# A graph attention kernel on one core: the maxima of heads 2 and 3 made apart, over four passes

## The chip, the core and the metric

The kernel runs on one core of a Trainium2 chip. The metric is the device time of one execution in microseconds (us); lower is better. TensorE multiplies matrices, VectorE, ScalarE and GpSimd do the element-wise work, and DMA queues move data between DRAM and the on-chip memory. In the profile they are PE (weight loads: PEld), DVE, ACT and POOL; SP is SyncE, which here only issues DMAs.

## The reference

Four layers follow each other on 1250 nodes of 1024 features: a graph attention with four heads, a block-sparse feed-forward layer with a large projection, a graph convolution, and a mixture of experts. Each has a layer norm ahead of it and is added to x. The change lies in the attention, which is

```python
def _L0_gnn_ref(h, W, a_l, a_r, src, dst):
    N, IN_FEAT, OUT_FEAT, HEADS, E = (1250, 1024, 256, 4, 20000)
    z = jnp.einsum('ni,hif->nhf', h, W)
    el = jnp.einsum('nhf,hf->nh', z, a_l)
    er = jnp.einsum('nhf,hf->nh', z, a_r)
    e = jax.nn.leaky_relu(el[src] + er[dst], 0.2)
    m = jax.ops.segment_max(e, dst, num_segments=N)
    ex = jnp.exp(e - m[dst])
    s = jax.ops.segment_sum(ex, dst, num_segments=N)
    alpha = ex / s[dst]
    out = jax.ops.segment_sum(alpha[:, :, None] * z[src], dst, num_segments=N)
    return out.reshape(N, HEADS * OUT_FEAT)
```

with h the layer norm of x. The maximum m of a destination node and head is the leaky ReLU of (the largest el over its sources, plus its er), since the leaky ReLU is monotonic.

## The kernel before

**The data.** The 1250 nodes are ten tiles (T) of 125 (R). The 20000 edges become a dense matrix of counts: CT holds it on chip with sources on the partitions, and nm_d in DRAM holds, for each tile of destinations, a mask of 125 destinations by 1250 sources that is 0 where there is an edge and -1e30 where there is none. Z holds the transformed features, with a column of ones behind each head's 256; Z of heads 0 and 1 lies in the buffer BZ, that of heads 2 and 3 in a tile of its own. el and er are the two halves of the scores.

**Maxima and bounds.** `maxima` (L336) goes over the ten tiles of destinations. For each it loads a tile nm of the mask (two DMAs on SP's queue, L106 and L107, 610 KB), and for both heads of a pair VectorE adds el, spread over the partitions (els), to the mask and takes the largest: one fused operation, L343, of 125 x 1250 for a head. It is a generator that stops after each, so that its work can be laid between other work. `bounds` (L347) turns the maxima of a pair of heads into two numbers for each destination (bd), which stand for the score less the maximum on the two branches of the leaky ReLU. `to_row` (L178) turns them by a TensorE transpose (L181) and a ScalarE copy to st (L183), and sends them to DRAM on POOL's queue (L185); `spread` (L188) loads them back, the same 2500 numbers for all 125 partitions (L190, 1220.7 KB), into rows[h], the tile rr. There are two rr buffers: head 2 takes the one of head 0, head 3 that of head 1.

**A pass.** `attend(h, b)` (L438) makes head h for the half b of the destinations, 625 of them. For each of ten source tiles, VectorE makes u from the rows and el (L443), ScalarE takes its exponential (L444), VectorE limits it and multiplies by the counts to w (L447), and TensorE multiplies w by Z into five accumulators of 125 x 257 (L449; in the profile each matmul of 32-bit data is two). At the end ScalarE copies the five sums of weights (L453), VectorE inverts them (L455, L456) and adds the scaled result to X (L459), which frees the accumulators: there are six, and a pass takes five. u and w have three buffers each.

The passes stand in the order (0,0), (0,1), (1,0), (1,1), (2,0), (3,0), (2,1), (3,1). `between` is stepped after each source tile of a pass:

```python
        with tc.tile_pool(name="mx1", bufs=1) as mxp:
            els1 = el_rows(1, mxp, tps)
            attend(0, 0)
            search = maxima(1, mxp, els1)
            attend(0, 1, search)
            attend(1, 0, search)
            bounds(1, mxp, tps, rowp)
            attend(1, 1)
```

So the 20 maxima of the second pair are made beside passes (0,1) and (1,0), one for each source tile, and the bounds of both heads follow together. The pool mx1 (nm, sc, els, top, bd, st) ends behind (1,1); the pool al, opened ahead of (2,0), holds the small tiles of the next layer norm (the statistics L503 among them) and takes the same memory.

**What sets the order.** The program's order isn't the order on the engines: a scheduler lays the instructions of each engine into one fixed queue when the kernel is built, and semaphores join the queues. An instruction waits for everything ahead of it on its own engine, a DMA for everything ahead of it on its issuing queue. SP's queue carries the mask tiles, and the weights of the projection (`load_weights`, L407) and of its small block-diagonal factors, the rails (`load_rails`, L412: maker L414 and up L415), which go into BZ as soon as heads 0 and 1 no longer need it. POOL's queue carries X, els, the rows of bounds and the products of the rails (L416, L418). TensorE multiplies the rails (L424). Behind the attention come the projection's matmuls (L595) by two levels of Strassen's scheme, then the graph convolution and the experts.

Of the kernel before, what the change touches and what calls it, by code (L numbers as in the profile page):

```python
# [8 lines left out]
F32 = mybir.dt.float32  # L9
# [10 lines left out]
P = 128  # L20
R, T = 125, 10
N = R * T
RA = 112
D = 1024
KD = D // P
# [10 lines left out]
NP = N + 2  # L36
NQ = NP // 4
HN, HT = N // 2, T // 2
# [60 lines left out]
def gnn_ffn_kernel(ctx, tc, x, src, dst, gat_w, a_l, a_r, maker, up, cproj,  # L99
# [98 lines left out]
    with tc.tile_pool(name="gw", bufs=1) as gwp, tc.tile_pool(name="gps", bufs=3, space=PSUM) as psp:  # L198
# [137 lines left out]
        def maxima(g, mxp, els):  # L336

            for d in range(T):
                nm = mxp.tile([R, N], F32, name="nm2", bufs=3 - g)
                dma(nc.sync, nm, nm_d[d])  # L340
                for h in (2 * g, 2 * g + 1):
                    sc = mxp.tile([R, N], F32, name="sc2")
                    nc.vector.tensor_tensor_reduce(sc, nm, els[:, h - 2 * g, :], scale=1.0, scalar=-3.0e38,  # L343
                                                   op0=ALU.add, op1=ALU.max, accum_out=mx[:, h, d:d + 1])
                    yield

        def bounds(g, pool, psp, rowp):  # L347

            hs = slice(2 * g, 2 * g + 2)
            for dst_t, f in ((el2, SLOPE), (el8, 1.0 - SLOPE)):  # L350
                nc.vector.tensor_scalar(dst_t[:, hs], el[:, hs], f, None, op0=ALU.mult)
            top = pool.tile([R, 2, T], F32, name="top")
            nc.vector.tensor_tensor(top, mx[:, hs], er[:, hs], op=ALU.add)
            nc.vector.scalar_tensor_tensor(top, top, SLOPE, top, op0=ALU.mult, op1=ALU.max)
            bd = pool.tile([R, 2, 2, T], F32, name="bd")
            nc.vector.tensor_tensor(bd[:, :, 0], er[:, hs], top, op=ALU.subtract)
            nc.vector.scalar_tensor_tensor(bd[:, :, 1], er[:, hs], SLOPE, top, op0=ALU.mult, op1=ALU.subtract)
            for h in range(2):
                rows[2 * g + h] = rowp.tile([R, 2, N], F32, name="rr", bufs=2)
                if 2 * g + h == 0:  # L360

                    for i in range(2):
                        for t0 in range(0, T, 4):
                            n = min(4, T - t0)
                            pb = psp.tile([P, 4, R], F32, name="pt")
                            for t in range(n):
                                nc.tensor.transpose(pb[:R, t, :], bd[:, h, i, t0 + t:t0 + t + 1].to_broadcast([R, R]),
                                                    ident[:R, :R])
                            copy = nc.vector.tensor_copy if t0 == 4 else nc.scalar.copy
                            copy(rows[0][:, i, t0 * R:(t0 + n) * R], pb[:R, :n, :].rearrange("p a b -> p (a b)"))  # L370
                    continue
                spread(rows[2 * g + h].rearrange("p a n -> p (a n)"),
                       to_row(pool, psp, bd[:, h].rearrange("p a t -> p (a t)"), 2 * T, f"bd{2 * g + h}"))
# [4 lines left out]
        with tc.tile_pool(name="mx0", bufs=1) as mxp:  # L378
            search = maxima(0, mxp, els0)
# [4 lines left out]
            bounds(0, mxp, psp, rowp)  # L384
# [50 lines left out]
    with tc.tile_pool(name="att", bufs=3) as atp, tc.tile_pool(name="aps", bufs=6, space=PSUM) as aps, \  # L435
# [25 lines left out]

        with tc.tile_pool(name="mx1", bufs=1) as mxp:
            els1 = el_rows(1, mxp, tps)
            attend(0, 0)
            search = maxima(1, mxp, els1)
            attend(0, 1, search)
            attend(1, 0, search)
            bounds(1, mxp, tps, rowp)
            attend(1, 1)
# [5 lines left out]
        xT = xTp.tile([P, KD, NP], F32, name="xT")  # L475
        for c in (HN, NP - 1):
            nc.gpsimd.memset(xT[:, :, c:c + 1], 0.0)
        with tc.tile_pool(name="al", bufs=2) as lnp:
            attend(2, 0)
# [770 lines left out]
```

## Time and profile before

| | us |
|---|---|
| median of 3 runs | 2926.47 (2922.64 to 2928.51) |
| the profiled execution | 2923.05, span 2921.3 |
| PE busy | 2857.7 (98%) |
| DVE busy | 1686.0 (58%) |
| ACT busy | 875.8 (30%) |
| POOL busy | 765.4 (26%) |
| 80 u (L443), attention only | 68.4, one 0.871 |
| 80 w (L447) | 64.3, one 0.809 |
| 20 maxima (L343) of heads 2 and 3 | 29.3, one 1.463 |
| 800 matmuls of the passes (L449) | 185.1 |

The busy time of an engine is the time from an instruction's start to its end, and successive instructions overlap a little, so starts are a better measure of a stretch than durations. A row of the timeline has the start, the length, the engine, the line, the operation with what it writes and reads, the number of instructions merged, and in brackets the engine's idle time ahead of it with what ended it. In the chain of work that ended last each step is followed back to what released it. The profile drops the digits of tile names, so nm2 is nm and sc2 is sc.

### The profile page before, as it was taken

What the parts mean: (1) busy time and instruction counts of PE and PEld (TensorE: products, weight loads), DVE (VectorE), ACT (ScalarE), POOL (GpSimd) and SP (SyncE); (2) the same over time, 40 slices, a digit from 0 to 9 for tenths busy, and PEclk for the clock granted to TensorE, in tenths of its full rate; (3) what the DMA queues carried; (4) which work ended last, traced back from release to release, by engine and by line L of the source; (5) the groups of instructions that cost most, each with busy time, mean ns of one, the idle gap of its engine ahead of it and who ended that gap; (6) DMA issues with size and microseconds to landing.
All of it is one profiled execution on the core that took longest, in us unless ns stands there. A gap on an engine that the chain in (4) does not pass through costs nothing.

```text
span 2921.3 us, 32800 instructions
## 1 busy us (share of the span) xinstructions
PE 2857.7 (98%) x11389; PEld 1892.0 (65%) x11389; DVE 1686.0 (58%) x2796; ACT 875.8 (30%) x1415; POOL 765.4 (26%) x994
## 2 busy tenths in 40 slices
PE   8999889999999999999999999999999999999998
PEld 5574777666766666666666667667667644445774
DVE  7686987855555565565465556455457665431114
ACT  2221234443343343343343443443440010010000
POOL 2000110224334334334334334344331100002001
PEclk9999999999999999999999999999999999999999
DMA  5245632569999999999999999999996502332655
GB/s 144 66 107 142 160 75 96 193 161 190 195 187 222 199 188 221 197 190 230 183 186 224 182 190 197 174 172 182 167 249 183 158 11 70 94 114 68 218 198 167
DMA packets 288438, 478.33 MB, mean 164 GB/s; under 512 B 75807, under 2 KB 159865, under 8 KB 287639
## 3 DMA queue, kind: packets, MB, share of 16 engines
q0 software_dynamic: 116176, 273.68, 52.9%
q1 hardware_dynamic: 172088, 202.44, 23.8%
q8 instruction: 95, 1.56, 0.2%
q14 instruction: 79, 0.65, 0.1%
HBM read 193.66 MB, written 282.34 MB: 163 GB/s over the span
## 4 chain that ended last, share of the span: by engine, by line
PE 80%; DMA 3%; DVE 2%; issue 0%; ACT 0%; POOL 0%; SPq 0%; DVEq 0%; ACTq 0%
PE po L595 55%; PE pab L1041 6%; PE ph L998 5%; PE po L866 4%; PE pz L429 3%; PE po L449 3%; PE po L1147 2%; DMA X<-in_gcn_w 2%; DMA yg<-ys_d,back 1%; PE pt L156 1%; PE pg L962 1%; DMA low<-in_gcn_w 1%; DMA rowbd<-st 0%; PE px L737 0%; PE pt L1137 0%
## 5 line engine op out<-in xcount | busy, mean ns | idle before, releaser
L608 POOL DMA_DIRECT2D acc_d<-low x686 | 594.6, 867 | 923.5 <-ACT low L604 895.6
L604 ACT COPY low<-po 128x626 f32<-128x626 f32 x735 | 501.2, 682 | 996.3 <-PE po L595 826.8
L595 PE MATMUL po<-X,arena 128*128 128x313 f32 x2144 | 603.5, 428 | 0.0
L595 PEld LDWEIGHTS po<-X,arena 128*128 128x128 f32 x2144 | 401.9, 189 | 170.2 <-issue 18.8
L595 PE MATMUL po<-low,arena 128*128 128x313 f32 x1584 | 449.2, 428 | 0.2 <-DVE low L588 0.2
L595 PEld LDWEIGHTS po<-low,arena 128*128 128x128 f32 x1584 | 296.8, 189 | 124.7 <-issue 13.2
L595 PE MATMUL po<-X,first_w 128*128 128x313 f32 x824 | 235.0, 429 | 0.9 <-DVE X L588 0.9
L595 PEld LDWEIGHTS po<-X,first_w 128*128 128x128 f32 x824 | 154.1, 189 | 67.0 <-issue 8.5
L595 PE MATMUL po<-X,BZ 128*128 128x313 f32 x648 | 185.8, 430 | 0.0
L588 DVE TENSOR_TENSOR X<-X 128x626 f32<-128x626 f32 x130 | 105.8, 816 | 111.1 <-PE po L595 88.2
L595 PE MATMUL po<-low,first_w 128*128 128x313 f32 x576 | 164.2, 428 | 0.9 <-DVE low L588 0.9
L595 PE MATMUL po<-low,BZ 128*128 128x313 f32 x552 | 158.4, 429 | 0.0
L595 PEld LDWEIGHTS po<-X,BZ 128*128 128x128 f32 x648 | 122.1, 191 | 50.7 <-issue 5.5
L212 PE MATMUL pz<-W,xT 128*125 128x512 f32 x320 | 141.2, 596 | 0.1
L595 PEld LDWEIGHTS po<-low,first_w 128*128 128x128 f32 x576 | 108.1, 189 | 45.8 <-issue 3.8
L595 PEld LDWEIGHTS po<-low,BZ 128*128 128x128 f32 x552 | 103.2, 189 | 44.5 <-issue 6.0
L588 DVE TENSOR_TENSOR X<-X,low 128x626 f32<-128x626 f32 x100 | 81.3, 814 | 79.8 <-PE po L595 65.2
L280 PE MATMUL pc<-os,od 125*125 125x417 f16 (+1 forms) x588 | 110.8, 344 | 4.9 <-issue 4.7
L449 PE MATMUL po<-BZ,w 125*125 125x257 f32 x400 | 95.6, 398 | 19.9 <-DVE w L447 18.8
L998 PE MATMUL ph<-low,first_w 125*125 125x512 f32 x250 | 109.5, 593 | 0.8 <-POOL tri L1066 0.8
L588 DVE TENSOR_TENSOR X<-low,X 128x626 f32<-128x626 f32 x88 | 70.9, 810 | 63.7 <-PE po L595 61.7
L588 DVE TENSOR_TENSOR low<-X,low 128x626 f32<-128x626 f32 x88 | 72.1, 820 | 60.6 <-PE po L595 59.6
(311 smaller groups left out, 3533.0 us busy)
## 6 DMA issues: line engine op xcount, KB each, us to landing
acc_d<-low POOLq DMA_DIRECT2D x735, 313.0 KB, 6.7
arena<-in_cproj SPq DMA_DIRECT2D x148, 256.0 KB
w<-in_w SPq DMA_DIRECT2D x16, 1024.0 KB
BZ<-in_cproj SPq DMA_DIRECT2D x56, 256.0 KB
first_w<-in_cproj SPq DMA_DIRECT2D x52, 256.0 KB
nm<-nm_d SPq DMA_DIRECT2D x20, 546.9 KB
w3t<-in_w SPq DMA_DIRECT2D x8, 1024.0 KB
X<-acc_d SPq DMA_DIRECT2D x19, 313.0 KB
```

The lines of the kernel that those rows point to most:

```text
L212: nc.tensor.matmul(pz, xT[:, k, t * R:(t + 1) * R], W[g][:, k], start=(k == 0), stop=(k == KD - 1))
L280: nc.tensor.matmul(pc[:, b, :nn], od[:, d - near[c][0], :], os[:, n0:n0 + nn], start=(c == win[d][0]), stop=(c == win[d][-1]))
L429: nc.tensor.matmul(pz, [*rail_parts(k)][-1][rows, :], xT[rows, (2 * b + k) % KD, n * NQ:(n + 1) * NQ], start=True, stop=True)
L449: nc.tensor.matmul(po[i], w[:, i * R:(i + 1) * R], Z[h // 2][:, s, h % 2, :], start=(s == 0), stop=(s == T - 1))
L588: tt(view(k), *a, op=ALU.add if sign == "+" else ALU.subtract)
L595: nc.tensor.matmul(po[:, o, :NQ], view(x)[:, q, o * P:(o + 1) * P], view(y)[:, q, :], start=(i == q == 0), stop=(i + 1 == len(pairs) and q ...
L604: nc.scalar.copy(part, po[:, :, :NQ])
L608: sent[:] = [nc.gpsimd.dma_start(out=acc_d[p - 1, i - 1], in_=part, accum_op=ALU.add).ins]
L866: nc.tensor.matmul(ph, block(a, x)[:, k, :], XS[W3[y, k]].rearrange("p q o -> p (q o)"), start=(k == 0), stop=(k == 3))
L998: nc.tensor.matmul(pa, cs[:, c, :], Y[FACTORS[p][1]][:, c], start=(c == 0), stop=(c == HT - 1))
L1041: nc.tensor.matmul(pab[:, :nn], w12[:, i, k, f * P:(f + 1) * P], rhs[:, k, n0:n0 + nn], start=(k == 0), stop=(k == KD - 1))
L1147: nc.tensor.matmul(po[:m, g, :], hid[:, f, s * P:s * P + m], w3t[:, f, g * 512:(g + 1) * 512], start=(f == 0), stop=(f == 1))
```

## The change

`maxima` now takes a list of heads instead of a pair, and so does `bounds`. Heads 0 and 1 are still made together. Heads 2 and 3 are made one by one: `search(2)` is stepped beside passes (0,1) and (1,0), with two steps for each maximum, and head 2's bounds follow behind (1,0); `search(3)` is stepped beside (1,1) and (2,0), two steps for each of its first five maxima and one for each of the others, so that head 3's bounds are written out after the sixth source tile of (2,0). Each head loads the ten mask tiles for itself: 20 loads of 610 KB in the place of ten. els and the two nm buffers stay as they were. The pool mx1 is now held to the end of (2,0), and the pool al is opened behind it; the tile xT and its two memsets, which came between the two pools, now come inside mx1.

```diff
@@ -333,55 +333,56 @@
                                                  start=(c == 0), stop=(c == EC - 1))
                         finish(d, pc)
 
-        def maxima(g, mxp, els):
+        def maxima(heads, mxp, els, bufs=2):
 
             for d in range(T):
-                nm = mxp.tile([R, N], F32, name="nm2", bufs=3 - g)
+                nm = mxp.tile([R, N], F32, name="nm2", bufs=bufs)
                 dma(nc.sync, nm, nm_d[d])
-                for h in (2 * g, 2 * g + 1):
+                for h in heads:
                     sc = mxp.tile([R, N], F32, name="sc2")
-                    nc.vector.tensor_tensor_reduce(sc, nm, els[:, h - 2 * g, :], scale=1.0, scalar=-3.0e38,
+                    nc.vector.tensor_tensor_reduce(sc, nm, els[:, h % 2, :], scale=1.0, scalar=-3.0e38,
                                                    op0=ALU.add, op1=ALU.max, accum_out=mx[:, h, d:d + 1])
                     yield
 
-        def bounds(g, pool, psp, rowp):
-
-            hs = slice(2 * g, 2 * g + 2)
+        def bounds(heads, pool, psp, rowp):
+
+            n = len(heads)
+            hs = slice(heads[0], heads[0] + n)
             for dst_t, f in ((el2, SLOPE), (el8, 1.0 - SLOPE)):
                 nc.vector.tensor_scalar(dst_t[:, hs], el[:, hs], f, None, op0=ALU.mult)
-            top = pool.tile([R, 2, T], F32, name="top")
+            top = pool.tile([R, n, T], F32, name="top")
             nc.vector.tensor_tensor(top, mx[:, hs], er[:, hs], op=ALU.add)
             nc.vector.scalar_tensor_tensor(top, top, SLOPE, top, op0=ALU.mult, op1=ALU.max)
-            bd = pool.tile([R, 2, 2, T], F32, name="bd")
+            bd = pool.tile([R, n, 2, T], F32, name="bd")
             nc.vector.tensor_tensor(bd[:, :, 0], er[:, hs], top, op=ALU.subtract)
             nc.vector.scalar_tensor_tensor(bd[:, :, 1], er[:, hs], SLOPE, top, op0=ALU.mult, op1=ALU.subtract)
-            for h in range(2):
-                rows[2 * g + h] = rowp.tile([R, 2, N], F32, name="rr", bufs=2)
-                if 2 * g + h == 0:
-
-                    for i in range(2):
+            for i, h in enumerate(heads):
+                rows[h] = rowp.tile([R, 2, N], F32, name="rr", bufs=2)
+                if h == 0:
+
+                    for j in range(2):
                         for t0 in range(0, T, 4):
-                            n = min(4, T - t0)
+                            w = min(4, T - t0)
                             pb = psp.tile([P, 4, R], F32, name="pt")
-                            for t in range(n):
-                                nc.tensor.transpose(pb[:R, t, :], bd[:, h, i, t0 + t:t0 + t + 1].to_broadcast([R, R]),
+                            for t in range(w):
+                                nc.tensor.transpose(pb[:R, t, :], bd[:, i, j, t0 + t:t0 + t + 1].to_broadcast([R, R]),
                                                     ident[:R, :R])
                             copy = nc.vector.tensor_copy if t0 == 4 else nc.scalar.copy
-                            copy(rows[0][:, i, t0 * R:(t0 + n) * R], pb[:R, :n, :].rearrange("p a b -> p (a b)"))
+                            copy(rows[0][:, j, t0 * R:(t0 + w) * R], pb[:R, :w, :].rearrange("p a b -> p (a b)"))
                     continue
-                spread(rows[2 * g + h].rearrange("p a n -> p (a n)"),
-                       to_row(pool, psp, bd[:, h].rearrange("p a t -> p (a t)"), 2 * T, f"bd{2 * g + h}"))
+                spread(rows[h].rearrange("p a n -> p (a n)"),
+                       to_row(pool, psp, bd[:, i].rearrange("p a t -> p (a t)"), 2 * T, f"bd{h}"))
 
         rows = {}
         rowst = ExitStack()
         rowp = rowst.enter_context(tc.tile_pool(name="rowp", bufs=1, side="right"))
         with tc.tile_pool(name="mx0", bufs=1) as mxp:
-            search = maxima(0, mxp, els0)
+            search = maxima((0, 1), mxp, els0, 3)
             for t in range(T):
                 for _ in range(3):
                     next(search, None)
                 z_tile(1, t)
-            bounds(0, mxp, psp, rowp)
+            bounds((0, 1), mxp, psp, rowp)
 
     XX = ctx.enter_context(tc.tile_pool(name="xpool", bufs=1)).tile([P, T, D], F32, name="X")
     X = XX[:R]
@@ -459,24 +460,33 @@
                 end = nc.vector.scalar_tensor_tensor(xs, po[i][:, :F], rs[:, i:i + 1], xs, op0=ALU.mult, op1=ALU.add)
             return end
 
+        def search(h, mxp, els):
+
+            for i, _ in enumerate(maxima((h,), mxp, els)):
+                yield
+                if i < 5 or h == 2:
+                    yield
+            bounds((h,), mxp, tps, rowp)
+
         with tc.tile_pool(name="mx1", bufs=1) as mxp:
             els1 = el_rows(1, mxp, tps)
             attend(0, 0)
-            search = maxima(1, mxp, els1)
-            attend(0, 1, search)
-            attend(1, 0, search)
-            bounds(1, mxp, tps, rowp)
-            attend(1, 1)
+            two, three = search(2, mxp, els1), search(3, mxp, els1)
+            attend(0, 1, two)
+            attend(1, 0, two)
+            next(two, None)
+            attend(1, 1, three)
 
             nc.vector.tensor_reduce(dis, deg.rearrange("p d s -> p s d"), AX.X, ALU.add)
             nc.vector.tensor_scalar(dis, dis, 1.0, None, op0=ALU.add)
             nc.scalar.activation(dis, dis, AF.Sqrt)
             nc.vector.reciprocal(dis, dis)
-        xT = xTp.tile([P, KD, NP], F32, name="xT")
-        for c in (HN, NP - 1):
-            nc.gpsimd.memset(xT[:, :, c:c + 1], 0.0)
+            xT = xTp.tile([P, KD, NP], F32, name="xT")
+            for c in (HN, NP - 1):
+                nc.gpsimd.memset(xT[:, :, c:c + 1], 0.0)
+            attend(2, 0, three)
+            next(three, None)
         with tc.tile_pool(name="al", bufs=2) as lnp:
-            attend(2, 0)
             nc.gpsimd.memset(m8, 1.0)
             nc.gpsimd.affine_select(m8, m8, pattern=[[-16, 8]], compare_op=ALU.is_ge, fill=0.0, base=0,
                                     channel_multiplier=1)
```

## The prediction

> **What bounds the kernel now.** First the page's chain of work that ended last, then the part of the span that the edit touches. Eight attention passes, each one head and one half of the destination nodes, run from 287 to 503 us.
>
> ```profile
> PE 80%; DMA 3%; DVE 2%; issue 0%; ACT 0%; POOL 0%; SPq 0%; DVEq 0%; ACTq 0%
> PE po L595 55%; PE pab L1041 6%; PE ph L998 5%; PE po L866 4%; PE pz L429 3%; PE po L449 3%; PE po L1147 2%; DMA X<-in_gcn_w 2%; DMA yg<-ys_d,back 1%; PE pt L156 1%; PE pg L962 1%; DMA low<-in_gcn_w 1%; DMA rowbd<-st 0%; PE px L737 0%; PE pt L1137 0%
> ```
>
> TensorE sets the end; the later work (L595 on) queues behind the attention, so time gained or lost before 503 us moves the end one for one. The stretches, one by one, show where attention itself isn't TensorE's:
>
> ```profile
> 330.00:378.00 48.00, 36.31 (x144) 27.86 (x142) 48.00 (x74) 10.45 (x22) 0.00 (x0) 0.93 0.38 106
> 378.00:403.00 25.00, 22.71 (x101) 18.43 (x102) 20.94 (x35) 9.81 (x15) 2.08 (x4) 1.00 0.66 165
> 431.00:454.00 23.00, 22.17 (x100) 18.58 (x100) 18.63 (x28) 8.47 (x16) 0.00 (x0) 1.00 0.00 1
> ```
>
> Columns: length, then busy time of PE, PEld, DVE, ACT, POOL, then PE clock, DMA share, GB/s. The third stretch is a pass that TensorE bounds: 23.0 us, VectorE busy 18.6. In the first VectorE has no gap: the 20 maxima of heads 2 and 3 (L343) lie there. The timeline around its end and the next stall:
>
> ```profile
> 374.34 1.47 DVE L343 CUSTOM_DVE_ANT_0 sc<-nm,els 125x1250 f32<-125x1250 f32 x1
> 376.51 0.19 DVE L353 TENSOR_TENSOR top<-mx,er 125x20 f32<-125x20 f32 x1
> 379.26 0.25 ACT L183 COPY st<-pt 20x125 f32<-20x125 f32 x1 [0.87 <-PE pt L181]
> 379.80 0.52 POOL L185 DMA_DIRECT2D rowbd<-st  x1 [66.97 <-ACT st L183]
> 381.90 0.53 POOL L190 DMA_DIRECT2D rr<-rowbd  x1 [1.59 <-DVE X L459]
> 392.87 0.69 DVE L503 BATCH_NORM_STATS2 st<-X 125x6 f32<-125x512 f32 x1 [3.95 <-DMA rowbd<-st]
> 407.40 0.85 PE L424 MATMUL pt<-BZ 128*128 128x128 f32 x4 [1.49 <-POOL BZ L418]
> 431.22 22.29 PE L449 MATMUL po<-Z,w 125*125 125x257 f32 x100 [0.92 <-DVE X L459]
> ```
>
> The reader is to see the trip of a head's bounds through DRAM (L183, L185, L190), a VectorE stop of 3.95 us and a rails stop of 1.49. From the second matmul of pass (0,1), 318.84, to that of (3,0), 431.22, are 112.4 us; four passes at 23.0 are 92.0. So 20.4 us is lost here, and that is all that can be won.
>
> **The change, part by part.** The built order of the instructions shows that it touches nothing before the fix-ups of pass (0,0) but two tiny VectorE operations, hidden in VectorE's 2.47 us wait before the first pass. From the first u of (3,0) every engine has its old order. So only the start of (3,0) counts.
>
> Price list (starts in VectorE's gapless stretches): u at L443 0.79, w at L447 0.75, a maximum 1.38 (350.82 to 352.20), the reciprocals and five updates of X that end a pass 2.4. Tried on the present stretch 330.36 to 376.51: 10 u, 12 w, 20 maxima, one end of pass: 7.9 + 9.0 + 27.6 + 2.4 = 46.9, measured 46.15, factor 0.984.
>
> *Maxima.* Still 20. The built order doesn't give five to each pass: the first stands where it stood, at 330.36, near the end of (0,1). From there to head 3's last bound VectorE has 29 u (nine of (1,0), all of (1,1) and (2,0)), 31 w (two of (0,1), ten, ten, nine), 20 maxima, three ends of pass and two sets of bounds at 0.38: 22.9 + 23.3 + 27.6 + 7.2 + 0.8 = 81.8, times 0.984 = 80.4. Head 3's bounds are ready at 410.8. VectorE bounds all of it: a pass with five maxima is 18.6 + 6.9 = 25.5 against TensorE's 23.0.
>
> *Head 2's bounds* come early in (1,1). Their rows need 0.9 (bounds to copied st) + 0.3 + 2.0 + 8.5 to 10.7 = 11.7 to 13.9 us. Six u, six w and three maxima stand on VectorE before the first u that reads them: (4.7 + 4.5 + 4.1) x 0.984 = 13.1. So 0 to 0.8 late; two mask loads keep that rr company, I take 0.5. Without the cover the price is all 13.
>
> *Head 3's bounds* come seven source tiles into (2,0), and (3,0) reads them at once. The chain, from the last bound: 0.9 to st (378.6 to 379.5); 0.4 because POOL's queue has two L418 multiplications (0.38 each) ahead of the row, which wait for VectorE's m2; 0.3 to issue; 2.0 until the second DMA starts (379.80 to 381.90, and 1.9 at 287.60); 8.5 for rr to land; 3.2 from first u to first matmul (289.34 to 292.55, likewise three u, then three w). Sum 15.3: 426.1. TensorE has eleven of (2,0)'s 50 matmul pairs left, 4.8, and transposes 0.4. It stops at 416.0 and idles ten us.
>
> The rr time is the unknown. Three rr DMAs landed in 8.5, 9.6 and 10.7, all in company (X loads or weights); els, as large, took 11.8. The Trainium skill, "DMA: Bandwidth & Descriptors", section on the anatomy of one DMA, has about 2.0 us plus bytes over 436 GB/s: 1.25 MB gives an estimate of 4.9. The trace never shows such a rate; with DMA engines full at 383 to 391 us it reads 187 to 291 GB/s. By the rule (3,0) would start at 422.5, by the row at 426.1. I take 8.5, the least crowded row, and keep 4.9 and 11.8 as ends.
>
> *Clock.* After an idle 4.9 us the first pass ran at half clock:
>
> ```profile
> 292.50:293.50 1.00, 0.95 (x2) 0.82 (x3) 1.00 (x2) 0.28 (x1) 1.00 (x3) 0.50 0.98 210
> 293.50:295.00 1.50, 1.50 (x5) 1.15 (x4) 1.50 (x3) 0.19 (x1) 0.66 (x2) 0.50 1.12 249
> 361.00:362.00 1.00, 1.00 (x4) 0.81 (x3) 1.00 (x3) 0.00 (x0) 0.00 (x0) 0.51 0.00 0
> ```
>
> Its first 26 matmuls took 7.67 instead of 26 x 0.217 = 5.64, so 2.0 lost; ten idle us cost the same. The last row is against the skill: "TensorE: Matmul & The Clock Gate", section on HAM oscillation, asks only that no idle gap passes about 3.4 us, and here the clock halved although no idle gap of TensorE's in the 15 us before passed 1.9 us. By the rule the VectorE-bound passes keep full clock and cost 0; by the row one or two drops may come, ten matmuls taking 3.91 for 2.43. VectorE hides this now, its next w starts 0.27 after them; with 2.5 us of margin per pass it mostly would again. I take 0, ends 0 and 1.5.
>
> *Loads of the mask* nm: ten more on SP, 610 KB each, two buffers. Now each is used 5.6 us after its buffer frees, and L343 never waits. In the new order that distance is 5.9 to 8.3 by the price list. Two loads run beside head 2's rr and may be late by 0 to 2 us; I take 0.5. SP's queue has one cproj load ahead of head 3's third mask that waits for (1,1)'s first tile, which is long done when that buffer frees. The other seven cproj loads now wait behind the last mask, are issued about 399 rather than 382 to 397, and feed nothing before 502. The maker and up loads stand ahead of the last two masks and wait only for (1,1) to end.
>
> *Pool mx1 held longer, al opened later:* the statistics that stopped VectorE 3.95 us now stand after head 3's bounds and wait some 3 us for their row; the ends of (2,0) behind them still finish about 3 us before rr lands. Cover gone, the price is those 3 us. The rails stop of 1.49 falls into the idle gap.
>
> *Sum.* Before, (3,0)'s gapless start is 431.22 - 0.43 = 430.8. After: 426.1 + 2.0 + 0.5 + 0.5 = 429.1, with X's updates already done so that the 0.92 gap isn't paid. Saved 1.7: the old loss shrinks by some twelve, a stall of ten and a cold clock come. The profiled execution, 2923.05 (span 2921.3), becomes 2921.4; the median, 2926.47, lies 3.4 higher, so the forecast is 2924.8. Within 0.2%, 5.9 us, is about what a measurement can't tell from no change.
>
> **Rivals.**
> *The mask loads become the bound (slower).* Place: two nm buffers, 18 loads that must land in the time between free and use. For it: twice the traffic beside rr and weights, and a distance of only 5.9 in places. Against: L343's idle is 0.0 now at 5.6, DMA share 0.38. It decides when landing runs 0.45 us past the distance on average: 18 x 0.45 = 8.1, in place of the 0.5, turns the gain into a loss of 5.9. At 0.6 past it: +8.6, 2935.1.
> *The row lands by the rule, and the gap shrinks (faster).* 4.9 for 8.5 gives 3.6 more: 2921.2; with nothing late at head 2's rows or the masks and VectorE one per cent quicker over its 80 us, 1.8 more: 2919.4. For it: nothing else is on the DMA queues then. Against: no rr here came under 8.5.
> *The spread is hidden outright.* Were no stall left, 10 + 2.0 - 0.9 more: 2913.7. Against: the built order leaves TensorE five us of work for a trip of fifteen. I give it little.
>
> **How the numbers follow.** Forecast case 0.70 (about 2920.5 to 2930 with its terms' ends and the scatter of the runs, 2922.64 to 2928.51); mask loads 0.15; quick row 0.12; hidden outright 0.03. The last two cross 5.9 us mostly: faster 0.14, slower 0.15, same 0.71. Eight in ten: from 2917.5, inside the quick row, to 2932, part of the mask case.
>
> **What would show it.** Right: VectorE gapless from about 330 to 410; a TensorE gap near 416 of some ten us with DMA rr<-rowbd of about 8.5 on the chain; PE clock 0.50 for about four us after; no 4 us wait of statistics before (2,0). Wrong: idle before L343 behind nm; that gap under six us or over thirteen; head 2's rows late, a gap at (2,0)'s start; clock drops that lengthen VectorE-bound passes.

## The result: 0.19% slower, and the profile after

The kernel after takes 2929.87 us (median of 20 runs, 2926.14 to 2941.92), the kernel before 2925.68 in the same session (20 runs). The ratio is 1.0019, with a 95% interval of 1.0012 to 1.0025: about 5.5 us slower. (The ratio isn't the quotient of the medians, which is 1.0014, or 4.2 us.) The forecast was 1.7 us faster. The profiled execution went from 2923.05 to 2927.98, its span from 2921.3 to 2926.3, so one pair of traces holds a difference of this size, 5.0 us.

The chain of work that ended last, of the kernel after:

```profile
PE 88%; issue 6%; DMA 3%; DVE 2%; POOL 1%; ACT 0%; SPq 0%; POOLq 0%; DVEq 0%; ACTq 0%
PE po L605 57%; PE pab L1051 6%; PE ph L1008 5%; PE po L876 4%; PE po L450 3%; PE pz L430 3%; PE pz L212 2%; PE pc L280 2%; PE po L1157 2%; PE pt L156 1%; DMA X<-in_x 1%; PE pg L972 1%; PE po L1168 1%; DMA nm<-nm_d 0%; DMA yg<-ys_d,back 0%
```

TensorE sets the end as before (L605 is the old L595). New in the list, though it rounds to nothing, is the mask load, nm<-nm_d. The same stretches as before, with the same columns, and the one between the second and third:

```profile
330.00:378.00 48.00, 42.89 (x187) 35.24 (x187) 46.20 (x76) 13.64 (x27) 0.52 (x1) 0.96 0.55 152
378.00:403.00 25.00, 19.49 (x76) 15.17 (x75) 19.45 (x31) 6.95 (x13) 1.97 (x5) 0.86 0.71 174
403.00:431.00 28.00, 19.78 (x92) 16.17 (x90) 21.26 (x38) 7.28 (x16) 5.37 (x10) 0.91 0.60 162
431.00:454.00 23.00, 20.92 (x89) 17.91 (x90) 19.02 (x24) 10.23 (x13) 0.00 (x0) 0.88 0.00 1
```

In the first stretch the change does what it says: TensorE is busy for 42.9 of 48 us instead of 36.3. The second gives it back. VectorE, which should have had no gap until 410, is busy for only 19.5 of 25 us; DMA share is 0.71 for 0.66 before. The timeline rows that answer to those shown of before:

```profile
373.21 0.16 DVE L357 TENSOR_TENSOR bd<-er,top 125x10 f32<-125x10 f32 x1
374.26 0.25 ACT L183 COPY st<-pt 20x125 f32<-20x125 f32 x1 [3.48 <-PE pt L181]
374.81 0.52 POOL L185 DMA_DIRECT2D rowbd<-st  x1 [61.76 <-ACT st L183]
380.39 0.53 POOL L190 DMA_DIRECT2D rr<-rowbd  x1 [5.07 <-DVE w L448]
389.14 0.87 DVE L444 SCALAR_TENSOR_TENSOR u<-rr,el 125x625 f32<-125x625 f32 x1 [2.54 <-DMA rr<-rowbd]
391.75 1.46 DVE L343 CUSTOM_DVE_ANT_0 sc<-nm,els 125x1250 f32<-125x1250 f32 x1 [1.74 <-DMA nm<-nm_d]
398.88 0.17 DVE L456 TENSOR_SCALAR rs<-rs 125x5 f32<-125x5 f32 x1 [1.27 <-ACT rs L454]
418.31 0.16 DVE L358 SCALAR_TENSOR_TENSOR bd<-er,top 125x10 f32<-125x10 f32 x1
419.65 0.54 POOL L185 DMA_DIRECT2D rowbd<-st  x1 [0.28 <-ACT st L183]
421.58 1.29 DVE L513 BATCH_NORM_STATS2 st<-X 125x6 f32<-125x512 f32 x2 [1.51 <-DMA rowbd<-st]
421.74 0.54 POOL L190 DMA_DIRECT2D rr<-rowbd  x1 [1.55 <-DMA rowbd<-st]
429.79 2.43 DVE L444 SCALAR_TENSOR_TENSOR u<-rr,el 125x625 f32<-125x625 f32 x3 [3.40 <-DMA rr<-rowbd]
433.08 25.26 PE L450 MATMUL po<-Z,w 125*125 125x257 f32 x106 [9.04 <-DVE w L448]
```

Read them in order. Head 2's bounds end at 373.4. The small row, 10 KB, leaves at 374.81, and the load that needs it leaves at 380.39: a trip of 5.6 us that took 2.1 before. So rr lands late, and VectorE stops for 2.54 us at (2,0)'s first u; then a mask is late by 1.74. Head 3's bounds end at 418.5, 7.7 us behind the forecast. From there on everything goes as forecast: the small row takes 2.1, rr 8.05, TensorE idles 9.04. The kernel after leaves (3,0) 4.8 us behind, (2,1)'s second matmul at 459.26 for 454.43, and keeps that to the end: its span is 5.0 longer.

The clock, in two windows of the kernel after (same columns, the clock is the last but two; the third window is the start of (1,0)):

```profile
393.90:398.70 4.80, 4.70 (x11) 3.74 (x12) 3.70 (x6) 2.04 (x7) 0.00 (x0) 0.50 0.56 141
433.00:440.30 7.30, 7.22 (x26) 6.05 (x27) 6.22 (x9) 3.32 (x5) 0.00 (x0) 0.76 0.00 0
344.50:350.50 6.00, 5.93 (x20) 4.95 (x21) 4.23 (x8) 0.44 (x1) 0.00 (x0) 0.73 0.64 196
```

TensorE ran out of work for 4.90 us when VectorE waited for head 2's rows, and its next ten matmuls took 4.65 us where ten take 2.43. That held (1,1)'s end up, and VectorE, which needs the sums, waited 1.27 more (the row at 398.88). The other two windows are the start of (3,0), after the stall of 9.04, and that of (1,0), where VectorE's w waited 1.20 and 0.57 us for TensorE to free its buffers.

### The profile page after: what moved, and what is told of

Same layout as the page of the kernel before. It is cut to its first block, busy times and chain, and to the rows that moved or that the text cites. A ratio compares the mean times of both kernels' runs of the same rounds, so it can differ in the third digit from the quotient of the medians.

```text
span 2926.3 us, 32840 instructions
## 1 busy us (share of the span) xinstructions
PE 2861.6 (98%) x11389; PEld 1895.8 (65%) x11389; DVE 1685.9 (58%) x2802; ACT 875.3 (30%) x1415; POOL 763.4 (26%) x994
## 4 chain that ended last, share of the span: by engine, by line
PE 88%; issue 6%; DMA 3%; DVE 2%; POOL 1%; ACT 0%; SPq 0%; POOLq 0%; DVEq 0%; ACTq 0%
PE po L605 57%; PE pab L1051 6%; PE ph L1008 5%; PE po L876 4%; PE po L450 3%; PE pz L430 3%; PE pz L212 2%; PE pc L280 2%; PE po L1157 2%; PE pt L156 1%; DMA X<-in_x 1%; PE pg L972 1%; PE po L1168 1%; DMA nm<-nm_d 0%; DMA yg<-ys_d,back 0%
## 5 line engine op out<-in xcount | busy, mean ns | idle before, releaser
L605 PE MATMUL po<-X,arena 128*128 128x313 f32 x2144 | 603.5, 428 | 0.0
L605 PEld LDWEIGHTS po<-X,arena 128*128 128x128 f32 x2144 | 401.9, 189 | 170.2 <-issue 18.8
L605 PE MATMUL po<-low,arena 128*128 128x313 f32 x1584 | 449.2, 428 | 0.0
L605 PEld LDWEIGHTS po<-low,arena 128*128 128x128 f32 x1584 | 296.8, 189 | 124.4 <-issue 12.8
L605 PE MATMUL po<-X,first_w 128*128 128x313 f32 x824 | 235.0, 429 | 0.0
L605 PEld LDWEIGHTS po<-X,first_w 128*128 128x128 f32 x824 | 154.1, 189 | 66.0 <-issue 8.5
L605 PE MATMUL po<-X,BZ 128*128 128x313 f32 x648 | 186.8, 432 | 0.0
L605 PE MATMUL po<-low,first_w 128*128 128x313 f32 x576 | 164.1, 428 | 0.0
L605 PE MATMUL po<-low,BZ 128*128 128x313 f32 x552 | 158.4, 429 | 0.0
L605 PEld LDWEIGHTS po<-X,BZ 128*128 128x128 f32 x648 | 122.7, 192 | 51.1 <-issue 6.2
L605 PEld LDWEIGHTS po<-low,first_w 128*128 128x128 f32 x576 | 108.1, 189 | 44.8 <-issue 3.8
L605 PEld LDWEIGHTS po<-low,BZ 128*128 128x128 f32 x552 | 103.2, 189 | 44.5 <-issue 6.0
L212 PEld LDWEIGHTS pz<-W,xT 128*125 128x125 f32 x320 | 59.1, 188 | 72.8 <-issue 70.0
```

Source lines behind the costliest of these rows:

```text
L212: nc.tensor.matmul(pz, xT[:, k, t * R:(t + 1) * R], W[g][:, k], start=(k == 0), stop=(k == KD - 1))
L605: nc.tensor.matmul(po[:, o, :NQ], view(x)[:, q, o * P:(o + 1) * P], view(y)[:, q, :], start=(i == q == 0), stop=(i + 1 == len(pairs) and q ...
```

## The experiments

Two readings serve in all of them. *The attention* is the time from (0,0)'s first matmul to (2,1)'s second, 161.88 us in the kernel before and 166.49 after, from one trace of each. *The row's trip* is the time from the issue of head 2's small row (rowbd) to the issue of its rr. Ratios are to the kernel before on the same chip.

| kernel | attention, us | row's trip, us | ratio, 95% interval |
|---|---|---|---|
| before | 161.88 | 2.1 | |
| after | 166.49 | 5.6 | 1.0019 [1.0012, 1.0025] |
| x_no_reload | 161.57 | 3.0 | 1.0007 [0.9999, 1.0015] |
| x_row_of_two | 158.81 | 5.0 | 0.9993 [0.9985, 1.0002] |
| x_both_costs | 153.67 | 3.0 | 0.9970 [0.9960, 0.9980] |
| x_before_bf16 | 161.00 | 2.1 | 0.9996 [0.9987, 1.0004] |
| x_after_bf16 | 161.41 | 2.1 | 1.0001 [0.9992, 1.0010] |
| x_after_weights_late | 165.13 | 4.0 | 1.0011 [1.0001, 1.0020] |
| x_rows_first | 161.94 | 2.1 | 1.0004 [0.9996, 1.0012] |
| x_three_masks | 158.66 | 5.1 | 0.9996 [0.9990, 1.0003] |
| x_three_bf16 | 158.32 | 3.1 | 0.9991 [0.9984, 0.9998] |
| x_early_before | 159.62 | 2.1 | 0.9995 [0.9986, 1.0004] |
| x_early_after | 175.22 | 5.3 | 1.0059 [1.0042, 1.0075] |
| x_early_three | 158.75 | 5.0 | 0.9997 [0.9986, 1.0009] |
| x_early_three_bf16 | 156.89 | 2.3 | 0.9990 [0.9981, 1.0000] |
| x_middle_three_bf16 | 153.30 | 3.6 | 0.9966 [0.9953, 0.9978] |

The second column agrees with the fourth: its difference to 161.88 gives each ratio's difference to 1 within 2.4 us, x_early_after's within 3.9. An interval reaches 2 to 4 us to either side (5 in x_early_after), so a time alone tells only larger differences apart. Two traces, of x_both_costs and x_middle_three_bf16, are of the slowest execution of their runs (2923.15 and 2921.32 us); these lost 7.7 and 7.4 us against the kernel before behind the attention, which the second column leaves out.

**Is it the mask loads?** Theory: ten more mask loads, three of which surround head 2's small row, delay that row and a mask, and so head 3's bounds. Rival: the stall ahead of (3,0) itself is dearer than priced. First the ten loads are left out:

```diff
-                nm = mxp.tile([R, N], F32, name="nm2", bufs=bufs)
-                dma(nc.sync, nm, nm_d[d])
+                if heads == (3,):
+                    nm = held[d % 2]
+                else:
+                    nm = mxp.tile([R, N], F32, name="nm2", bufs=bufs)
+                    dma(nc.sync, nm, nm_d[d])
+                    held[:] = [*held, nm][-2:]
```

> The changed kernel without the ten mask loads of head 3: its maxima are taken from the last two masks that head 2 loaded, so head 3's maxima are not the true ones; all 20 maxima, both sets of bounds and both trips of rows stay. Theory A (the second set of mask loads crowds the DMA engines while head 2's rows travel): the small row lands in about 2 us instead of 5.5, the rr behind it in about 8.5, VectorE waits for neither, head 3's bounds end near 411 instead of 418.5, pass (3,0) starts near 426 instead of 433, and the time is about 2922.5 (ratio to before 0.999). Rival B (head 2's row is late for another reason, the cproj load or a wait on VectorE): row still 5.5, bounds near 418, time 2929 to 2930 (ratio 1.0015).

Measured: 2924.57 us for 2923.37 of the kernel before. Its rows (VectorE's L343 isn't among them: nothing waits for a mask):

```profile
378.59 0.52 POOL L185 DMA_DIRECT2D rowbd<-st  x1 [63.91 <-ACT st L183]
381.58 0.53 POOL L190 DMA_DIRECT2D rr<-rowbd  x1 [2.47 <-DVE w L453]
410.92 0.17 DVE L362 SCALAR_TENSOR_TENSOR bd<-er,top 125x10 f32<-125x10 f32 x1
414.71 0.54 POOL L185 DMA_DIRECT2D rowbd<-st  x1 [15.52 <-ACT st L183]
429.71 25.87 PE L455 MATMUL po<-Z,w 125*125 125x257 f32 x106 [7.08 <-DVE w L453]
```

The row's trip is 3.0 us, and VectorE has no gap from 353 to 411: the waits for head 2's rr, for the mask and for the end of (1,1) are gone. Head 3's bounds end at 411.1. That this is close to the forecast's 410.8 is chance, since the built order changed with the edit: three u and two w fewer stand ahead of the last bound, and the passes begin at 294.93 and not at 292.77. Counted from the first matmul, the bounds come 9.5 us earlier than in the kernel after; 4.1 of them are waits that are gone, and nearly all the rest is the order. But only about 3.5 us came through to the time (4.9 to the attention): TensorE's turning of the bounds stands in a fixed place in its queue, and with bounds this early it comes late, so the row left 3.6 us after the bounds and not 1.2, and (3,0) began 18.6 us after the bounds and not 14.6.

**The stall ahead of (3,0) alone.** Head 3's rows are filled from head 2's, so that nothing waits for the last bounds:

```diff
+            rows[3] = rowp.tile([R, 2, N], F32, name="rr", bufs=2)
+            spread(rows[3].rearrange("p a n -> p (a n)"), row2[0])
```

> The changed kernel, but the rows of head 3 are loaded behind pass (1,1) from head 2's row in DRAM, so pass (3,0) and (3,1) use head 2's bounds; head 3's maxima, bounds and small row are still made. It prices the wait of (3,0) for head 3's rows. If the stall and the half clock behind it cost what the profile shows (9.0 idle plus 1.9, less the 0.9 gap at a pass's start): 10 us under the changed kernel, about 2920 (ratio to before 0.998). If something else would end last there (VectorE with its maxima, or this rr taking the DMA engines from the masks): gain under 5 us, 2925 or more.

Measured: 2921.51 for 2923.37, about 7.6 us under the kernel after. The trip of head 2's row is still 5.0 us, with the same stops behind it (rr 1.73, nm 2.04 and 0.64, TensorE 4.38 us idle and then at half clock). The gain is less than the stall of 9.04 and the clock's 1.9: with the stall gone TensorE still waits 1.10 us for (3,0)'s first w, and the added rr load at 388.2 runs beside the masks, with head 3's bounds 1.2 us later, counted from the first matmul.

**Do the two add up?** Both edits at once:

> The kernel after with both costs taken away at once: head 3's ten mask loads left out (its maxima use the last two masks of head 2) and head 3's two rows filled from head 2's row behind (1,1), so that (3,0) doesn't wait for head 3's trip. Its result is not the reference's. Alone the first brought about 3.5 us and the second 7.6 against the kernel after. If the two costs add up as the prediction's sum had it (mask loads and late rows ahead of the stall, then the stall): 11 us or more under the kernel after, ratio to the kernel before 0.998 or less (2917 to 2914). If the stall only took over what the masks had cost (the second hidden in the first): 7 to 8 us, ratio 0.9993.

Measured: 2916.08 for 2923.76, 0.9970: some 14 us under the kernel after (0.0049 of 2924; 12.8 by the attention), no less than 3.5 and 7.6 together. They are two separate costs: neither hides the other. (2,0) and (3,0) now follow each other without a stop of more than 1 us.

**Half the bytes.** The mask holds only 0 and -1e30, so BF16 does; every mask load is halved, and all of the computation stays. The kernel before with it is the yardstick:

```diff
-    nm_d = dram.tile([T, R, N], F32, name="nm_d")
+    nm_d = dram.tile([T, R, N], BF16, name="nm_d")
```

> The kernel before with the mask (nm, nm_d, nm2: 0 or -1e30) held in BF16, which halves its bytes: ten mask loads of 0.3 MB for 0.6. Whole computation. It is the yardstick for the next two kernels. In the kernel before no maximum waits for a mask, so in the attention it should bring nothing; the mask's writing in the counting phase changes a little. Expected within 2 us of the kernel before (ratio 0.9993 to 1.0007), L343 at 1.38 us per start-to-start as before; if a maximum over a BF16 mask is quicker, the stretch from 330 to 378 us is shorter by 20 times the difference.

> The kernel after with the mask in BF16. Whole computation. Theory A (the mask loads crowd head 2's rows): rowbd2 to rr2 falls from 5.6 to about 3 to 4 us, the stops of VectorE on rr2, nm and rs (7.3 us in sum) shrink to under 3, head 3's last bound comes 4 to 7 us earlier than 418.5 against the first u of (2,0), and the time falls by 3 to 6 us against the kernel after, to about 1.0003 of the kernel before plus what the BF16 mask alone does. Rival B (the row is late for another reason, for instance that VectorE itself is simply longer with ten more maxima apart): the row's trip stays at 5 us or more and the time at 1.0015 to 1.0025.

Measured: 2922.47 for the yardstick (0.9996, within the noise), 2923.41 for the kernel after with it (1.0001), where the kernel after has 1.0019. The rows of the latter:

```profile
367.79 0.52 POOL L185 DMA_DIRECT2D rowbd<-st  x1 [53.89 <-ACT st L183]
369.89 0.53 POOL L190 DMA_DIRECT2D rr<-rowbd  x1 [1.59 <-DVE rs L457]
407.71 0.16 DVE L358 SCALAR_TENSOR_TENSOR bd<-er,top 125x10 f32<-125x10 f32 x1
426.22 26.07 PE L450 MATMUL po<-Z,w 125*125 125x257 f32 x106 [7.07 <-DVE w L448]
```

The trip is 2.1 us, VectorE waits for neither rr of head 2 nor any mask, and the attention takes 161.41 us for the yardstick's 161.00: the cost of 4.6 is down to 0.4. A maximum over a BF16 mask takes as long as before (1.38 from start to start), so this isn't VectorE's gain. But the halving isn't the only difference, since the schedule shifted with the types: the row leaves 7 us earlier, the first weight load (374.5) stands behind it, and head 3's last bound has three u and three w fewer ahead of it. Two mask loads, at 365.9 and 368.9, stand on either side of the row, yet it had the DMA engines to itself: their busy share is 0.04 in the 1.3 us from its issue, where it is 0.86 in the kernel after from 374.8 to 377.0. Where BF16 masks do run beside the row, in x_three_bf16 and x_middle_three_bf16 further down (a share of 0.61 from 368.5 to 370.3 and of 0.55 from 367.2 to 369.4), the trip is 3.1 and 3.6 us.

**Masks or weights?** One load of the projection's weights leaves at 372.85, just ahead of two masks (head 3's third and fourth; the expectation below calls them its first two). Here all eight are issued behind the last mask:

```diff
-            for o in ("11", "12"):
-                for i in corner:
-                    load_weights(0, o, i)
+            with tc.issue_after(mask[0].ins):
+                for o in ("11", "12"):
+                    for i in corner:
+                        load_weights(0, o, i)
```

> The kernel after with the eight weight loads of the next stage (cproj) issued on SP's queue behind the last mask; in the kernel after one of them, 372.85 us, goes out just ahead of head 3's first two masks and of head 2's small row. Whole computation; the order of VectorE stays but for a few maxima that move by one instruction. If that weight load is what delays the small row: rowbd2 to rr2 falls from 5.6 to 3 us or less, the time by 3 us or more. If the mask loads are (in the run without head 3's masks seven cproj loads kept the row company and it took 3.0): the trip stays at 4.5 us or more and the time within 2 us of the kernel after (ratio to the kernel before 1.001 to 1.0025).

```profile
375.21 0.52 POOL L185 DMA_DIRECT2D rowbd<-st  x1 [61.69 <-ACT st L183]
379.20 0.53 POOL L190 DMA_DIRECT2D rr<-rowbd  x1 [3.47 <-DVE u L445]
388.18 0.87 DVE L445 SCALAR_TENSOR_TENSOR u<-rr,el 125x625 f32<-125x625 f32 x1 [1.18 <-DMA rr<-rowbd]
390.60 1.46 DVE L343 CUSTOM_DVE_ANT_0 sc<-nm,els 125x1250 f32<-125x1250 f32 x1 [1.55 <-DMA nm<-nm_d]
```

The answer lies between the two: the trip is 4.0 us, neither 3 nor 4.5. Of the 3.5 us that the row lost, the weight load has some 1.6 and the masks the rest, by this one trace. It is the cleanest pair, since as many u, w and maxima as in the kernel after stand ahead of head 3's last bound: VectorE's waits up to it fall from 7.4 to 4.5 us, and (3,0) starts 2.6 us earlier, counted from the first matmul. In time, 2925.79 for 2924.53 (1.0011), the run can't be told from the kernel after: the intervals overlap.

**Was the old stop of 3.95 us a cost?** The change also took away the 3.95 us for which VectorE's statistics waited. Before, with both small rows sent ahead of both rr, the stop goes too, and nothing else is changed:

```diff
-                spread(rows[2 * g + h].rearrange("p a n -> p (a n)"),
-                       to_row(pool, psp, bd[:, h].rearrange("p a t -> p (a t)"), 2 * T, f"bd{2 * g + h}"))
+                sent[h] = to_row(pool, psp, bd[:, h].rearrange("p a t -> p (a t)"), 2 * T, f"bd{2 * g + h}")
+            for h, row in sent.items():
+                spread(rows[2 * g + h].rearrange("p a n -> p (a n)"), row)
```

> The kernel before with both small rows sent to DRAM ahead of both rr loads (two st buffers); the computation is whole. The statistics that stop VectorE for 3.95 us wait for the second small row, which there stands behind an rr load. Expected: that wait goes, 3.5 to 4 us faster, about 2922 (ratio 0.9988). If TensorE had another wait just behind (the rails at 407): nothing, 2926.

Measured: 2924.22 for 2923.37, the same time, though the row with 3.95 is gone. The row of pass (2,0), before and then here:

```profile
408.09 22.21 PE L449 MATMUL po<-Z,w 125*125 125x257 f32 x100
407.35 23.90 PE L451 MATMUL po<-Z,w 125*125 125x257 f32 x100
```

Counted from the first matmul (292.55 and 293.43), the pass comes 1.6 us earlier, not 3.95: the rest TensorE had covered with w in store. Then its clock falls, to a mean of 0.64 from 407.3 to 412.0, the pass takes 1.7 us longer, and the gain is gone. So the stop was worth 1.6 us at most; whether the clock falls there in every run isn't known, but the times show no gain.

**A third mask buffer.** The sum is written over the mask, which frees the room, and head 3's maxima all go beside (1,1):

> The changed kernel with a third mask buffer (the sums of a maximum are written over the mask) and head 3's maxima all beside pass (1,1); the computation is whole. VectorE's queue then has head 3's bounds after the fifth to sixth source tile of (2,0). By the price list (25 u, 26 w, 20 maxima, three ends of pass, two sets of bounds: 74.9 x 0.984 = 73.7 behind 330.4) that is 404 us if no row or mask is late; the chain of 15 ends at 419 and TensorE has until about 418 to work: almost no stall, (3,0) near 420, time about 2917 (ratio 0.996). If head 2's rows are as late as in the changed kernel (theory A holds and the traffic is the same): 5 to 7 more, 2922 to 2924.

Measured: 2921.67 for 2923.37, close to the second of the expected cases. Head 3's bounds end at 406.1 (404 expected), but rr still comes 3.46 us late for (3,0), and the small row of head 2 is as slow as in the kernel after, 5.1 us. With BF16 as well:

> Whole computation, a candidate to beat both kernels: the third mask buffer, head 3's maxima all beside (1,1), and the mask in BF16. In the built order head 3's bounds now stand behind the second u of (2,0) and not its sixth, so their rows have about 3 us more; with F32 masks (3,0) waited 3.5 us for its rows and lost 1.4 to the clock, at ratio 0.9996. Expected: no wait of (3,0) for rr, rowbd to rr 3 us or less for head 2, ratio to the kernel before 0.9975 to 0.9985 (2916 to 2919) if the BF16 mask alone is worth nothing. If the row's trip doesn't speed up or VectorE bounds (1,1) all the same, 0.999 to 1.

Measured: 2920.70 for 2923.76, 0.9991, short of what was expected; (3,0) waits no more, but one mask of head 3 comes 3.93 us late, with weight loads between the masks on SP's queue.

**An earlier start.** The first maximum starts at 330 us: els is asked for behind all the loads of X on POOL's queue, at 312.3 us, and lands at 324.1. My theory by now was that this late start was the root of it, with head 3's maxima squeezed against (3,0):

```diff
-    for t in range(T):
-        dma(nc.gpsimd, X[:, t, :], x_t[t])
...
             els1 = el_rows(1, mxp, tps)
+            for t in range(T):
+                dma(nc.gpsimd, X[:, t, :], x_t[t])
             attend(0, 0)
```

> The kernel before with one move: the row els of heads 2 and 3 is asked for ahead of the ten loads of X on POOL's queue, not behind them (it was issued at 314 us, landed 326, and no maximum could start before 330). Whole computation. In the built order the 20 maxima now stand from the seventh u of (0,0) to (2,0)'s first u, in 24 source tiles and not in 15. A pass has 23.0 - 18.6 = 4.4 us to spare on VectorE, so 2.4 passes hide 10.6 of 27.6 us; lost are 17 of the 20.4 lost now, and the 20 tile loads of masks run beside X and head 1's row. Expected 3 to 6 us faster: ratio 0.998 to 0.999. If els lands so late that VectorE stops in (0,0), or X comes too late for (0,0)'s end: 1.000 or more.

> The kernel after with the same one move (els ahead of the X loads). Whole computation. In the built order the maxima now stand in every pass from (0,0) to the third source tile of (2,0), head 2's rows have ten source tiles until they are read, and head 3's bounds come behind (1,1)'s updates, five source tiles into (2,0). Theory (what went wrong was the late start of the maxima, which pushed head 3's bounds against (3,0) and head 2's row among the mask loads): 3.9 passes hide 17 of 27.6 us, lost are 10.5 plus 0 to 4 for head 3's rows, so 6 to 10 us under the kernel before: ratio 0.9966 to 0.998, and faster than the kernel before with the same move. Rival (splitting the heads costs by itself, with ten more mask loads): slower than the kernel before with the same move.

> Whole computation, a candidate: els ahead of the X loads, the third mask buffer, head 3's maxima all beside (1,1). Head 3's bounds stand at the third u of (2,0), 8 source tiles ahead of (3,0). Expected: no stall at (3,0); 3.4 passes hide 15 of 27.6 us, lost 12.6 and not 20.4: 7 to 8 us under the kernel before, ratio 0.9972 to 0.9977.

> The same with the mask in BF16 and the eight weight loads of the next stage (cproj) issued behind the last mask, since in the BF16 run without the move four of them stood between the masks on SP's queue and a mask came 3.9 us late. Whole computation. Expected 0 to 3 us faster than the run with F32 masks: ratio 0.9965 to 0.9977; no wait of L343 for nm.

Measured, for 2923.85 of the kernel before: 2921.59, 2939.13, 2923.79 and 2920.89. All four missed what was expected of them. The theory fell, and plainest where it promised most. The kernel after with the early start:

```profile
306.84 1.46 DVE L343 CUSTOM_DVE_ANT_0 sc<-nm,els 125x1250 f32<-125x1250 f32 x1 [6.41 <-DMA els<-rowel]
319.96 1.46 DVE L343 CUSTOM_DVE_ANT_0 sc<-nm,els 125x1250 f32<-125x1250 f32 x1 [4.92 <-DMA nm<-nm_d]
324.86 1.46 DVE L343 CUSTOM_DVE_ANT_0 sc<-nm,els 125x1250 f32<-125x1250 f32 x1 [1.93 <-DMA nm<-nm_d]
332.57 1.46 DVE L343 CUSTOM_DVE_ANT_0 sc<-nm,els 125x1250 f32<-125x1250 f32 x1 [3.23 <-DMA nm<-nm_d]
```

els itself came 6.4 us late, and then the masks came late one after the other, beside the X loads: 10.1 us on these three rows. The kernel before with the same move waits for els nearly as long (5.79) and for no mask at all, since it loads each mask once for two heads, twice as far apart. Between these two, 1.0059 and 0.9995, the only difference is the change itself, and it costs some 19 us there (0.0064 of 2924; 15.6 by the attention) for 5.5 in its own place. That is the rival of the theory, the doubled mask loads.

**The version that beats both.** Three BF16 masks, weights behind the masks, and els asked for behind five of the ten X loads:

> Whole computation, the last candidate: three masks in BF16, head 3's maxima beside (1,1), weights behind the masks, and els asked for behind five of the ten X loads, so that maxima can start at the end of (0,0) without stopping VectorE there (asked for ahead of all X loads it cost a stop of 5.5 to 6.4 us). In the built order the first maximum stands at the tenth u but one of (0,1)'s first half, head 2's bounds at (1,1)'s first u, head 3's at (2,0)'s second. Expected: els landed by 316 us and no stop for it, 3 to 5 us under the run with three BF16 masks alone: 2916 to 2918 where the kernel before has 2923.8, ratio 0.997 to 0.998. If els is late again or the masks crowd the X loads: 0.9985 to 1.000.

Measured: 2915.27 us (six runs) for 2924.53, 0.9966 [0.9953, 0.9978]. Its rows:

```profile
316.44 1.46 DVE L343 CUSTOM_DVE_ANT_0 nm<-nm,els 125x1250 bf16<-125x1250 bf16 x1 [0.44 <-DMA els<-rowel]
370.84 0.53 POOL L190 DMA_DIRECT2D rr<-rowbd  x1 [3.10 <-DVE X L459]
422.12 22.29 PE L449 MATMUL po<-Z,w 125*125 125x257 f32 x100 [0.69 <-DVE X L459]
```

The first maximum stands at 316 and waits 0.44, no mask is waited for, and (3,0) begins without a stall. Against the run with three BF16 masks alone the attention is 5.0 us shorter. How much of this the earlier start brings isn't shown: the weights behind the masks came with it, and the 3.93 us for which that run waited for a mask are gone as well. An earlier start with the weights behind the masks but els ahead of all X loads (x_early_three_bf16) is 3.6 us longer.

## Why the prediction was wrong, step by step

**Loads of the mask and Head 2's bounds: these failed.** The prediction gave each 0.5 us. Measured are 2.54 us of VectorE for head 2's rr, 1.74 for a mask and 1.27 for the end of (1,1) behind the TensorE stop that came of it: 5.6 where 1.0 stood. Of the 11.7 to 13.9 us that head 2's rows were to need, 2.0 was the small row, taken from two trips in the trace of before, neither of which had a mask load beside it. The steps asked whether the *large* load would be slow in company (8.5 to 10.7; it took 8.7) and never whether the small one would. With mask loads around it, it took 5.6. All sixteen traces show the same: 2.1 to 3.6 us where the masks were absent, already loaded or halved, 4.0 to 5.6 with whole ones near.

**Clock: right in size, incomplete in place.** Two us after the stall were forecast; the 24 matmuls behind it took 7.11 instead of 5.2, so 1.9. (The prediction calls the clock at 361 us against the skill; it set it against one section's rule on long idle gaps, and no run here tests what short ones do.) But drops within the passes were priced at 0, with ends 0 and 1.5, on the ground that VectorE had 2.5 us of margin. TensorE, at a mean clock of 0.73 at the start of (1,0), held VectorE up by 1.20 and 0.57 us at 348.6 and 350.0. In this stretch, which VectorE bounds, these waits made head 3's bounds later.

These five waits sum to 7.3 of the 7.7 us by which head 3's bounds were later than 410.8; 0.2 more was there before the first pass. 7.7 less the 1.0 allowed, less 0.7 by which the chain behind was shorter (14.6 for 15.3), less 0.1 of the clock, is 5.9 of the 6.5 us between forecast and trace at (2,1). The other 0.6 lies within (3,0) and isn't explained.

**Maxima: right.** From the first maximum to head 3's last bound the kernel after takes 87.8 us (330.66 to 418.47), of which VectorE waits 7.4. That leaves 80.4, which is what the price list and its factor gave. The order and the number of instructions stood as described.

**Head 3's bounds: right.** 0.3 to issue, 2.1 for the row, 8.05 for rr, 3.3 to the first matmul; TensorE idle 9.04 for the forecast ten. The row's 8.5 was the better guide than the estimate of 4.9 us from the Trainium skill, "DMA: Bandwidth & Descriptors", section on the anatomy of one DMA: with only 82 KB of other loads beside it, rr took 8.05.

**Pool mx1 and al: right in effect, but for a reason missed.** The wait of the statistics is now 1.51 and is hidden. That losing the old 3.95 brings no time, the run with the rows first shows; the prediction counted it in the 20.4 us that could be won.

**The rivals.** "The mask loads become the bound" had the right resource and the wrong door. It looked at the two buffers and asked whether 18 loads would each be 0.45 us late; in the kernel after one mask was late, and the harm went through the small row. Where X loads keep the masks company, in the run with the early start, it came about as written. The outright hiding and the quick row did not come. The time, 2929.87, lies inside the range, and even at the upper end of the forecast case (2920.5 to 2930, 70 in 100); but that width stood for the terms' ends and the scatter of the runs. Against the kernel before, the sign was wrong.

**Two readings that don't hold.** A pass that TensorE bounds takes 23.2 us from second matmul to second matmul (431.22 to 454.43); 23.0 was the length of the window. So 19.5 us could be won and not 20.4. And DMA rates near 436 GB/s do occur: the last microsecond of the stretch from 383 to 391 has 356 GB/s and not at most 291, and that from 521 to 522 has 432. Neither enters the sum.

**How the masks delay the small row.** The traces' records of single DMA packets show most of it. The row is ten packets of 1000 bytes. In the kernel after each took 0.06 to 0.10 us, no longer than before (0.05 to 0.10), but they started 2.2 to 3.4 us behind the issue, where before it was 1.1 to 1.2. So they weren't slowed; they waited, while the DMA engines were at work on packets of 5000 bytes of the masks (0.29 us each) and 1024 bytes of the weights (0.05 us). In the run without head 3's masks, with weight packets alone beside them, they started after 1.3 to 1.6. This is 2.2 of the 3.5 us. The other 1.3 lies behind the last packet: until rr was issued 2.2 us passed, before 0.9.

**Still open.** Why the time behind the last packet grew isn't shown. And the weight load's share of 1.6 us is one trace against one.

## What to carry to other kernels

Price a small transfer by the company it will have, not by the row in which it travelled alone: 10 KB took 2.1 us or 5.6, and all that follows it in a dependent chain moves with it. When an edit makes a load more often, look at every other transfer in that stretch and not only at the reader of the load. And when VectorE is made the bound of a stretch, the waits that were free in it become the cost.

## What the hardware showed that was not expected

- A DMA of 10 KB to DRAM took 4.0 to 5.6 us from its issue to the issue of the load behind it with whole mask loads (0.6 MB, in rows of 5000 bytes) beside it, but 3.0 us with three weight loads of 256 KB issued from 376.6 to 379.8, around its start at 378.6 (the run without head 3's masks).
- TensorE ran at a granted clock of 0.50 after an idle time of 4.9 us (393.9 to 398.7), and the cost went on: ten matmuls 2.2 us longer, VectorE's next step 1.27 later.
- els (1.25 MB) asked for right behind head 1's rr, as large, and ahead of three tiles of X took 14.5 us to land (292.3 to 306.8), where 8.05 was measured for an rr with 82 KB of other loads beside it.
